# A two-layer graph network on one core: owner matrices kept as bytes, transposes placed behind z, z's weights loaded last

## The chip, the cores and the metric

One Trainium2 chip, one of its cores. The metric is device time in microseconds from the first to the last instruction of the program, with what lies around it; it is given as the median of several runs. A core has TensorE (PE, matrix products; its weight loads are a row of their own, PEld), VectorE (DVE), ScalarE (ACT), GpSimd (POOL) and SyncE (SP). They run side by side, each in the order of its own instructions. DMA transfers are issued from the queues of SP, ACT and POOL.

## The reference

A layer of attention over a graph and a layer of neighbour means, each with a residual sum and a layer norm. There are 4096 nodes with 512 features; `adj` is 4096 x 4096 int32, with about four ones in a row.

```
Wh   = einsum('nf,hfo->hno', x, W)                    # 8 heads of 64
f1   = einsum('hno,ho->hn', Wh, a[:, :64]);  f2 likewise with a[:, 64:]
e    = where(adj > 0, leaky_relu(f1[:, :, None] + f2[:, None, :], 0.2), -9e15)
x1   = layernorm(x + softmax(e) @ Wh)                 # layer 0, heads side by side

agg  = (adj > 0) @ x1 / max(deg, 1)
out  = relu(concat(x1 @ W_self + b_self, agg @ W_nb + b_nb) @ W_comb + b_comb)
y    = layernorm(x1 + out)                            # layer 1
```

## The kernel before, in words

The adjacency is so sparse that the kernel turns each row into a short list of neighbours and gathers rows from DRAM, instead of multiplying with 4096 x 4096 matrices. Nodes are cut into 32 blocks of 128 (`NB`). If a row or a block has more neighbours than the lists hold, a flag sends the program to a dense version, which does not run with these inputs.

Three of a node's neighbours have slots of their own (`K0`). The others of a block share 2 x 128 slots (`KH`): each such slot belongs to one node, its owner. Two 0/1 matrices say who owns what: `of` (kept as bytes for all blocks, slot by node, widened to `st` when used) and the owner matrix `own`, its counterpart, which is made on VectorE when a block needs it: `owners` compares a row of numbers with the owner's number of each slot, twice per block. In layer 1 the same function also scales by 1/degree.

The order of work is written out by hand (`manual_schedule`): every engine runs its instructions in the order in which the Python code issues them. Generators (`decode`, `mean_row`, `fold_weights`) cut longer pieces of work into steps, and `some(...)` or `next(...)` places a step. There are three stages:

1. *Lists and node rows.* For each block b, SyncE loads the adjacency (2 MB in two halves, four buffers `at`), ScalarE turns each half into a 0/1 mask (L379), TensorE folds the masks into keys (`fold_adj`), VectorE takes the largest keys (`max_keys`). Every fourth block a `decode` turns four blocks of keys into neighbour lists `idx` and the `of` matrices (a ScalarE copy to bytes, L470). Beside this `node_block` computes Wh and both attention terms for one block of nodes (L321) and `store` writes them to the DRAM table `t0`. Node blocks run at the pace of the adjacency loop over `LB` = 30 blocks; at b = 12 (`AHEAD`) there is one extra. The two last adjacency blocks and node block 31 are handled after the loop.
2. *Attention.* A software pipeline over i: while block i is normed, block i + 1 is weighed and summed, block i + 2 gets its softmax terms and block i - 1 is multiplied with `m2`. `gather` (L519) issues five indirect DMAs per block from GpSimd, `GA` = 5 blocks deep. On TensorE a block needs: four transposes of its normed rows (`transposed`, L313, then copied by ScalarE, L315), the small products `a_reach` (L569) and `a_shared_sum` (L550), the product with the owner matrix (`a_shared`, L596) and z (`a_z`, L633). z goes to the DRAM table `t1` (L638), 32 stores on SyncE's queue.
3. *Output.* The same kind of pipeline over `t1`, with gathers of five DMAs per block and `GB` = 7 buffers: products with `m1` (L657) and with the scaled owner matrix (L664), ReLU, residual, norm, store.

`m2` and `m1` are products of a weight matrix with its half of `W_comb` (`fold_weights`: four transposes and four products for each of four chunks, L261 and L272). For `m2` the weights (2 MB, `load_fold`) are loaded inside the adjacency loop at b = 28, ahead of adjacency block 30; the fold is spread over the hand-over from stage one to stage two. `fold_bias` (L290) adds four bias terms on VectorE. `m1` is folded between stages two and three.

Around the change, an iteration i of stage two issues, in this order: moments(i), gather(i + 4), transposes(i - 1), reach(i + 1), the widening of `of`, weighing of i + 1, softmax terms of i + 2, root and norm of i, z(i - 1), the rest of the sums of i + 1, the small sum of i + 2, the owner product of i + 1, the owner matrix of i + 3.

In stage three the first gathers stand ahead of the loop:

```
    G1 = {b: gather(t1, b, gps) for b in range(GA)}
    gps += [... for k in range(GA, GB)]
    G1[GA] = gather(t1, GA, gps)
    ...
    for b in range(NB):
        ...
        if b + GB - 1 < NB:
            G1[b + GB - 1] = gather(t1, b + GB - 1, gps)
```

Of the kernel before, what the change touches and what calls it, by code (L numbers as in the profile page):

```python
# [55 lines left out]
GB = 7  # L56
# [31 lines left out]
def listed_layers(  # L88
# [33 lines left out]
    AHEAD = 12  # L122
# [97 lines left out]
    of = const.tile([P, NB, KH * P], U8, name="of")  # L220
    idx = const.tile([P, NB, KS], U32, name="idx")
# [32 lines left out]
    def fold_weights(loaded, m, wp, tag):  # L254
# [12 lines left out]
        for c in range(FB):  # L267
            nxt = turned(c + 1) if c + 1 < FB else None
            yield
            mp = ps.tile([P, HD], F32, name=tag, bufs=2)  # L270
            for d in range(FB):
                nc.tensor.matmul(  # L272
                    mp, lhsT=wT[:, d, :], rhs=wc[:, d, :], start=(d == 0), stop=(d == FB - 1)
                )
            yield
            nc.scalar.copy(m[:, c, :], mp)
            wT = nxt
# [9 lines left out]
    def fold_bias(loaded, bcol):  # L287

        for d in range(FB):
            nc.vector.scalar_tensor_tensor(  # L290
                brow, loaded[1][:, d, :], bcol[:, d : d + 1], brow, OP.mult, OP.add
            )

# [120 lines left out]
    def decode(b0, dp, place, slow=False):  # L414
# [49 lines left out]
        for b in range(b0, b0 + G):  # L464
# [5 lines left out]
            nc.scalar.copy(of[:, b, :], st)  # L470
            sts.append(st)
            if slow or b == b0 + G - 1:
                yield
        pe = ps.tile([P, G, KH, EX + H], F32, name="sm", bufs=2)
# [23 lines left out]
        nc.vector.tensor_scalar(idx[:, bs, K0:KS], jx, float(N + 1), None, OP.min)  # L498

    def owners(b, pool, scaled=False):  # L500

        s = pool.tile([P, KH, P], F32, name="own", bufs=4)
        for k in range(KH):
            E = es[:, b, k, :]
            if scaled:
                nc.vector.tensor_scalar(
                    s[:, k, :], iota[:, 1 : P + 1], E[:, KX + 2 : KX + 3],
                    E[:, KX + 1 : KX + 2], OP.is_equal, OP.mult,
                )
            else:  # L510
                nc.vector.tensor_scalar(
                    s[:, k, :], iota[:, 1 : P + 1], E[:, KX + 2 : KX + 3], None, OP.is_equal
                )
# [16 lines left out]
    def a_owners(b, wp):  # L530
        OWN[b] = owners(b, wp)
# [160 lines left out]
    wp = ctx.enter_context(tc.tile_pool(name="work", bufs=1))  # L692
    dp_cm = tc.tile_pool(name="decode", bufs=1, side="right")
    dp = dp_cm.__enter__()
    fp_cm = tc.tile_pool(name="fold", bufs=1, side="right")
    fp = fp_cm.__enter__()
# [75 lines left out]
    def on_last(b):  # L772
        return sp.tile([P, KH * P], F32, name="last", bufs=G)

    def store(w, row, eng=nc.scalar):
        eng.dma_start(t0[2 + w * P : 2 + (w + 1) * P, :], row[:, 0:TW])
# [5 lines left out]
    for b in range(LB):  # L782
        for k in range(1 + (b == AHEAD)):
            load_x(w + k + XL)
            sum_x(w + k + XL, xacc)
        if b + 2 < LB:
            load_adj(b + 2, ap)
        elif b + 2 == LB:
            loaded = load_fold(1, w_nb, fp)
            load_adj(LB, ap)  # L790
# [6 lines left out]
        nxt = transposed(w + 1, wp)  # L797
# [8 lines left out]
        if b == AHEAD:  # L806
# [10 lines left out]
        if b % G == G - 1:  # L817
            lists = [*lists[-1:], decode(b + 1 - G, dp, on_own)]
    row = node_block(w, xT)
    store(w, row)  # L820
    key_bank(LB)
    for h in range(NH):
        mask_adj(LB, h)
    fold_adj(LB - 1, dp)
    max_keys(LB - 1)
    row = node_block(w + 1, nxt)
    store(w + 1, row, nc.sync)
    load_adj(LB + 1, ap)
# [3 lines left out]
    gps = [ctx.enter_context(tc.tile_pool(name=f"gat{k}", bufs=1)) for k in range(2)]  # L832
    for b in range(2):
        G0[b] = gather(t0, b, gps)
    m2s = fold_weights(loaded, m2, wp, "pw")
    some(lists)
    fold_adj(LB, dp)
    max_keys(LB)
    next(m2s)
    key_bank(LB + 1)  # L840
    some(lists)
    for k in range(3):
        next(m2s)
    mask_adj(LB + 1, 0)
    a_owners(0, wp)
    fold_bias(loaded, bcol)
    some(lists)
    mask_adj(LB + 1, 1)
    next(m2s)
    fold_adj(LB + 1, dp)  # L850
    max_keys(LB + 1)
    next(m2s)
    ap_cm.__exit__(None, None, None)
    bp_cm.__exit__(None, None, None)
    wq = ctx.enter_context(tc.tile_pool(name="work2", bufs=1))
    a_owned(0, wq)
    gps += [ctx.enter_context(tc.tile_pool(name=f"gat{k}", bufs=1)) for k in range(2, GA)]
    sp_cm = tc.tile_pool(name="last", bufs=1, side="right")
    sp = sp_cm.__enter__()
    lists = [decode(NB - G, dp, on_last, slow=True)]  # L860
    some(lists)
# [4 lines left out]
    for i in range(-2, NB + 2):  # L866
# [4 lines left out]
        if on(i - 1):  # L871
            xT = transposed(i - 1, wp)
        if on(i + 1):
            a_reach(i + 1)
        if i == -1:
# [13 lines left out]
        if i == -2:  # L889
            next(m2s)  # L890
            some(lists)
        if on(i):
            norm(i, xs[:, i, :])
        if on(i - 1):
            a_z(i - 1, xT, wp)
        if on(i + 1):
            a_adds(i + 1, wq)
        if on(i + 2):
# [6 lines left out]
        if i == 1:  # L905
            loaded = load_fold(0, w_self, fp)
            brw = load_bias(0)
        if i == -1:
            next(m2s, None)
        if 2 <= i < 12:  # L910
            some(lists)
        if i == 12:
            sp_cm.__exit__(None, None, None)
            m1_pool = ctx.enter_context(tc.tile_pool(name="m1", bufs=1))
            m1 = m1_pool.tile([P, FB, HD], F32, name="m1")
    bcol = bias_column(0, brw)
    fold_bias(loaded, bcol)
    for _ in fold_weights(loaded, m1, wp, "nm"):
        pass
# [3 lines left out]
    fp_cm.__exit__(None, None, None)  # L923
# [6 lines left out]
    for b in range(2):  # L930
        OWN[b] = owners(b, wp, scaled=True)
# [22 lines left out]
    for b in range(NB):  # L954
# [13 lines left out]
        if b + 2 < NB:  # L968
            OWN[b + 2] = owners(b + 2, wp, scaled=True)
# [400 lines left out]
```

## Time and profile before

| | us |
|---|---|
| median of three runs | 802.6 (797.52 to 804.33) |
| the profiled execution, its own time | 717.85 |
| its span | 716.1 |
| TensorE busy | 636.6 (89%) |
| VectorE busy | 492.2 (69%) |
| ScalarE busy | 453.3 (63%) |
| GpSimd busy | 361.6 (50%) |
| mean granted TensorE clock | 0.960 |

The rows of groups give a line of the code, the engine, the operation, what it writes and reads, how often it ran, its busy time, the mean of one in ns, and the idle time of its engine just before, with what ended it. The costliest that the change touches or meets:

```profile
L519 POOL DMA_INDIRECT g<-t,idx x320 | 305.8, 956 | 166.9 <-issue 75.3
L633 PE MATMUL pw<-m,xT 128*128 128x512 f32 x256 | 122.1, 621 | 12.3 <-ACT xT L315 12.3
L315 ACT COPY xT<-tp 128x512 f32<-128x512 f32 x80 | 46.5, 581 | 81.7 <-PE tp L313 80.7
L584 DVE TENSOR_TENSOR g<-g,key 128x1024 f32<-128x1024 f32 x64 | 77.8, 1216 | 1.1
```

A product of 32-bit floats appears as two matmul records, so z's four products are eight rows. In rows of the timeline the columns are start and duration in us, then engine, line and operation; a bracket holds the idle time of that engine just before, and who ended it. The profiled execution is shorter than the runs of the median by 84.75 us.

### The profile page before, as it was taken

To read this page: it belongs to the slowest core of one execution; us is meant where nothing else is said; L and a number is where in the kernel's file an instruction comes from. 1 tells how busy PE (TensorE), PEld (TensorE's weight loads), DVE (VectorE), ACT (ScalarE), POOL (GpSimd) and SP (SyncE) were. 2 spreads that over 40 slices of the span, in tenths; PEclk is the share of its full clock that TensorE was granted. 3 is DMA by queue.
4 is the path that set the end of the run, shared out by engine and by line. 5 is a ranking of instruction groups with operands and counts; after the bars stand their busy time and mean duration, and the time that the engine had idled before them with its cause. 6 is when DMAs were issued, how large, how long until landed. Compare 5 with 4: busy or idle time off the path is not lost. (4 is left out here: it accounts for less than half of the span.)

```text
span 716.1 us, 8935 instructions
## 1 busy us (share of the span) xinstructions
PE 636.6 (89%) x2454; PEld 362.1 (51%) x2454; DVE 492.2 (69%) x1431; ACT 453.3 (63%) x947; POOL 361.6 (50%) x403
## 2 busy tenths in 40 slices
PE   3797898988998789978999999999999999999963
PEld 1565666756665444435555555554444444444421
DVE  5256777766867778999899999983135655666552
ACT  3477786777867526645666575664346876777753
POOL 6512123121000777655576666400777777777771
PEclk9989999999999968999999999999999999999996
DMA  9999999999998878876688878611678888888883
GB/s 280 384 350 393 393 393 394 394 390 392 343 394 305 263 213 275 294 206 189 186 226 231 233 226 234 190 45 44 191 210 261 262 248 256 258 265 249 257 246 119
DMA packets 84262, 191.26 MB, mean 267 GB/s; under 512 B 12513, under 2 KB 12521, under 8 KB 84206
## 3 DMA queue, kind: packets, MB, share of 16 engines
q0 software_dynamic: 25600, 84.56, 40.6%
q1 hardware_dynamic: 53952, 97.53, 37.2%
q10 hardware_dynamic: 4654, 8.54, 3.2%
q8 instruction: 21, 0.34, 0.2%
q14 instruction: 35, 0.29, 0.1%
HBM read 165.29 MB, written 25.31 MB: 266 GB/s over the span
## 5 line engine op out<-in xcount | busy, mean ns | idle before, releaser
L519 POOL DMA_INDIRECT g<-t,idx x320 | 305.8, 956 | 166.9 <-issue 75.3
L379 ACT ACTIVATE ab<-at 128x2048 bf16<-128x2048 int32 x64 | 122.1, 1909 | 43.6 <-DMA at<-in_adj_dram 39.1
L321 PE MATMUL pw<-w_sb,xT 128*128 128x264 f32 x512 | 137.9, 417 | 0.1
L633 PE MATMUL pw<-m,xT 128*128 128x512 f32 x256 | 122.1, 621 | 12.3 <-ACT xT L315 12.3
L321 PEld LDWEIGHTS pw<-w_sb,xT 128*128 128x128 f32 x512 | 99.1, 204 | 29.0 <-issue 3.6
L307 POOL TENSOR_TENSOR xacc<-xacc,xs 128x512 f32<-128x512 f32 x32 | 41.1, 1285 | 123.2 <-DMA xs<-in_x_dram 122.7
L315 ACT COPY xT<-tp 128x512 f32<-128x512 f32 x80 | 46.5, 581 | 81.7 <-PE tp L313 80.7
L633 PEld LDWEIGHTS pw<-m,xT 128*128 128x128 f32 x256 | 47.4, 195 | 63.5 <-issue 48.3
L584 DVE TENSOR_TENSOR g<-g,key 128x1024 f32<-128x1024 f32 x64 | 77.8, 1216 | 1.1
L596 PE MATMUL nm<-g,own 128*128 128x512 f32 x128 | 64.5, 628 | 0.0
L313 PEld LDWEIGHTS tp<-ident,xs 128*128 128x128 f32 x320 | 40.5, 147 | 38.3 <-issue 31.5
L657 PE MATMUL nm<-m,xT 128*128 128x512 f32 x128 | 57.7, 593 | 1.5 <-ACT xT L315 1.5
L313 PE MATMUL tp<-ident,xs 128*128 128x128 f32 x320 | 50.9, 284 | 7.9 <-DMA xs<-in_x_dram 7.4
L657 PE MATMUL pw<-m,xT 128*128 128x512 f32 x128 | 57.6, 592 | 0.0
L325 DVE COPY row<-pw 128x264 f32<-128x264 f32 x64 | 27.1, 424 | 43.1 <-PE pw L321 26.4
L671 DVE SCALAR_TENSOR_TENSOR sm<-y,lst,nm 128x512 f32<-128x512 f32 x16 | 12.1, 755 | 43.7 <-PE nm L664 43.7
L664 PE MATMUL nm<-g,own 128*128 128x512 f32 x64 | 32.0, 625 | 5.9 <-DMA g<-t,idx 5.9
L647 DVE TENSOR_TENSOR sm<-sm,g 128x512 f32<-128x512 f32 x32 | 22.2, 694 | 19.5 <-ACT sm L643 19.5
L657 PEld LDWEIGHTS nm<-m,xT 128*128 128x128 f32 x128 | 23.1, 190 | 24.6 <-issue 23.0
L671 DVE SCALAR_TENSOR_TENSOR sm<-y,lst,pw 128x512 f32<-128x512 f32 x16 | 12.1, 756 | 34.0 <-PE pw L664 34.0
L657 PEld LDWEIGHTS pw<-m,xT 128*128 128x128 f32 x128 | 23.1, 190 | 23.4 <-issue 23.4
L664 PE MATMUL pw<-g,own 128*128 128x512 f32 x64 | 30.3, 595 | 2.0 <-DMA g<-t,idx 2.0
(177 smaller groups left out, 1007.5 us busy)
## 6 DMA issues: line engine op xcount, KB each, us to landing
at<-in_adj_dram SPq DMA_DIRECT2D x64, 1024.0 KB, 10.7
t<-row SPq DMA_DIRECT2D x32, 256.0 KB, 3.5
out_dram<-row SPq DMA_DIRECT2D x32, 256.0 KB, 3.9
t<-row ACTq DMA_DIRECT2D x31, 260.0 KB, 5.8
xs<-in_x_dram SPq DMA_DIRECT2D x31, 256.0 KB, 11.2
g<-t,idx POOLq DMA_INDIRECT x320, 4.2
wc<-in_L_gnn_W_comb_dram SPq DMA_DIRECT2D x2, 1024.0 KB, 16.7
w_sb<-in_L_gnn_W_dram SPq DMA_DIRECT2D x8, 128.0 KB, 4.4
```

The costliest lines, as they stand in the source:

```text
L307: nc.gpsimd.tensor_tensor(xacc, xacc, xs[:, b, :], OP.add)
L313: nc.tensor.transpose(tp[:, c, :], xs[:, b, ts(c, P)], ident)
L315: nc.scalar.copy(t, tp)
L321: nc.tensor.matmul(pw, lhsT=xT[:, c, :], rhs=w_sb[:, c, k * HW : (k + 1) * HW], start=(c == 0), stop=(c == FB - 1),)
L325: nc.vector.tensor_copy(row[:, k * HW : (k + 1) * HW], pw)
L379: nc.scalar.activation(ab, loads.pop((b, h)), AF.Relu, accum_out=asum[:, b, h : h + 1])
L519: nc.gpsimd.indirect_dma_start(out=g[:, k, 0 : table.shape[1]], out_offset=None, in_=table[:, :], in_offset=bass.IndirectOffsetOnAxis(ap=i ...
L584: nc.vector.tensor_tensor(gv if to is None else to.rearrange("p (k h d) -> p k h d", k=1, h=H), gv, E[b][:, sl].unsqueeze(3).to_broadcast( ...
L596: nc.tensor.matmul(NM[b], lhsT=OWN[b][:, k, :], rhs=G0[b][:, K0 + k, H:TW], start=False, stop=(k == KH - 1), skip_group_check=True,)
L633: nc.tensor.matmul(pz, lhsT=xT[:, c, :], rhs=m2[:, c, :], start=(c == 0), stop=(c == FB - 1))
L657: nc.tensor.matmul(NM[b], lhsT=xT[:, c, :], rhs=m1[:, c, :], start=False, stop=False, skip_group_check=True,)
L664: nc.tensor.matmul(NM[b], lhsT=OWN[b][:, k, :], rhs=g[:, K0 + k, 0:HD], start=False, stop=(k == KH - 1), skip_group_check=True,)
```

## The change

- The owner matrices of stage two are no longer made on VectorE for each block. `decode` gets one more step, which makes those of four blocks at once, as bytes (`own`, in a tile that lives through the kernel); `a_owners` is now a ScalarE copy that widens a block's bytes to 32-bit floats. `owners` stays for stage three, always scaled.
- `decode`'s copies to `of` are issued after its loop; for the first six decodes they run on GpSimd, for the last two on ScalarE.
- In stage two the transposes of block i are issued behind z(i - 1) and the sums of i + 1, and used by z(i) in the next iteration. Before, they were issued at the start of the iteration that uses them.
- A second extra node block runs at b = 6, so that all of the loop's blocks end with node block 30, and node block 31 follows directly. All 32 adjacency blocks are loaded in the loop's order; z's weights are loaded behind them. `store` is always on ScalarE's queue.
- `fold_weights` stops after every second product, and its steps are spread over the start of stage two; `fold_bias` stops after every term.
- The last four lists' decode begins earlier, in a tile of the pool of the weights. The weights of `m1` are loaded at i = 12 instead of i = 1, and `m1` is written over the tile of its own weights.
- `GB` is 6 instead of 7. The lines ahead of the loop of stage three that gather blocks 0 to 5 are as before.

```diff
-GB = 7
+GB = 6
-    AHEAD = 12
+    AHEAD = (6, 12)
+    own = const.tile([P, NB, KH, P], U8, name="own8")
@@ fold_weights
-            yield
+                if d % 2:
+                    yield
@@ decode
-            nc.scalar.copy(of[:, b, :], st)
+        for g in range(G):
+            if b0 + G < LB - G:
+                nc.gpsimd.tensor_copy(of[:, b0 + g, :], sts[g])
+            else:
+                nc.scalar.copy(of[:, b0 + g, :], sts[g])
...
+        yield
+        nc.vector.tensor_tensor(
+            own[:, bs].rearrange("p g k c -> p (g k) c"),
+            iota[:, 1 : P + 1].unsqueeze(1).to_broadcast([P, G * KH, P]),
+            es[:, bs].rearrange("p g k c -> p (g k) c")[:, :, KX + 2 : KX + 3].to_broadcast(
+                [P, G * KH, P]
+            ),
+            OP.is_equal,
+        )
@@ a_owners
-        OWN[b] = owners(b, wp)
+        OWN[b] = wp.tile([P, KH, P], F32, name="own", bufs=4)
+        nc.scalar.copy(
+            OWN[b].rearrange("p k c -> p (k c)"), own[:, b].rearrange("p k c -> p (k c)")
+        )
@@ the loop of stage one
-        if b + 2 < LB:
-            load_adj(b + 2, ap)
-        elif b + 2 == LB:
-            loaded = load_fold(1, w_nb, fp)
-            load_adj(LB, ap)
+        load_adj(b + 2, ap)
...
+    loaded = load_fold(1, w_nb, fp)
     row = node_block(w, xT)
     store(w, row)
@@ the hand-over
+    gps = [ctx.enter_context(tc.tile_pool(name="gat0", bufs=1))]
+    G0[0] = gather(t0, 0, gps)
     m2s = fold_weights(loaded, m2, wp, "pw")
     some(lists)
+    for b in (LB, LB + 1):
+        key_bank(b)
+        for h in range(NH):
+            mask_adj(b, h)
+        some(lists)
+        fold_adj(b, dp)
+        max_keys(b)
...
+    lists = [decode(NB - G, dp, on_last, slow=True), *lists[-1:]]
+    for k in range(3):
+        some(lists)
+    for k in range(4):
+        next(m2s)
@@ the loop of stage two
-        if on(i - 1):
-            xT = transposed(i - 1, wp)
...
         if on(i - 1):
-            a_z(i - 1, xT, wp)
+            a_z(i - 1, XT.pop(i - 1), wp)
+        if i == -2:
+            some(lists)
         if on(i + 1):
             a_adds(i + 1, wq)
+        if on(i):
+            XT[i] = transposed(i, wp)
...
+        for k in range({-2: 1, -1: 3, 0: 2}.get(i, 0)):
+            next(m2s, None)
+        if 1 <= i < 12:
+            some(lists)
+        if 1 <= i < 5:
+            next(biased)
+        if i == 12:
+            loaded = load_fold(0, w_self, fp)
+            brw = load_bias(0)
```

## The prediction

> **What bounds the kernel now.** I read the busy time by stage first, then a steady stretch of the second stage in order of time, then the GpSimd queue from 455 us on, then the hand-over between first and second stage. The stages: masks, keys and node rows to 228; hand-over to 274; attention and z to 498; fold of the second weights to 528; output blocks to 716.
>
> ```profile
> core 0: us, PE busy (x) PEld busy (x) DVE busy (x) ACT busy (x) POOL busy (x), PEclk, DMA share, GB/s
> 4.00:228.00 224.00, 191.69 (x1025) 135.58 (x1026) 151.90 (x580) 159.91 (x209) 52.40 (x68) 0.95 1.03 378
> 228.00:274.00 46.00, 37.46 (x125) 20.42 (x123) 34.58 (x103) 20.39 (x45) 32.94 (x34) 0.81 0.77 232
> 274.00:498.00 224.00, 208.62 (x747) 112.66 (x745) 193.80 (x498) 135.33 (x363) 121.18 (x128) 0.99 0.67 200
> 498.00:528.00 30.00, 28.53 (x88) 13.96 (x87) 7.26 (x20) 10.47 (x21) 20.52 (x22) 1.00 0.61 184
> 528.00:716.00 188.00, 170.20 (x475) 79.31 (x473) 102.50 (x218) 125.73 (x310) 131.34 (x139) 0.96 0.77 241
> ```
>
> Stage one is full of DMA (share 1.03). The hand-over leaves TensorE half slow (clock 0.81). In the second stage TensorE (93%) and VectorE (87%) are both nearly full; a steady block shows how they meet:
>
> ```profile
> 411.27 0.60 PE L313 MATMUL tp<-ident,xs 128*128 128x128 f32 x4
> ...
> 411.71 0.51 PE L569 MATMUL sm<-dn,st 128*128 128x8 f32 x4
> ...
> 411.91 0.59 ACT L315 COPY xT<-tp 128x512 f32<-128x512 f32 x1 [2.01 <-PE tp L313]
> ...
> 412.54 3.70 PE L633 MATMUL pw<-m,xT 128*128 128x512 f32 x8 [0.33 <-ACT xT L315]
> ...
> 416.08 0.51 PE L550 MATMUL sm<-e,own 128*128 128x8 f32 x4
> ...
> 416.44 1.96 PE L596 MATMUL nm<-g,own 128*128 128x512 f32 x4
> ...
> 417.92 0.43 DVE L511 TENSOR_SCALAR own<-iota,es 128x128 f32<-128x128 f32 x2
> ...
> 418.25 0.60 PE L313 MATMUL tp<-ident,xs 128*128 128x128 f32 x4
> ...
> 418.44 0.69 DVE L612 SCALAR_TENSOR_TENSOR y<-y,nm 128x512 f32<-128x512 f32 x1
> ```
>
> The period is 418.25 - 411.27 = 6.98 us. TensorE idles 0.33 of it: z needs the ScalarE copy of the transposes, which begins only when they end, and only the small product at 411.71 lies between. VectorE has no gap over 0.1 us, and its last item, the owner matrix, holds it from 417.92 to 418.44, 0.52 us. So two limits of almost one length stand side by side; taking one away alone would gain little.
>
> In stage three the limit is another:
>
> ```profile
> 501.08 0.97 POOL L519 DMA_INDIRECT g<-t,idx  x1 [41.56 <-DVE brow L290]
> 502.35 0.94 POOL L519 DMA_INDIRECT g<-t,idx  x1 [0.30 <-issue]
> ...
> 698.76 3.75 PE L664 MATMUL nm<-g,own 128*128 128x512 f32 x4 [4.97 <-DMA g<-t,idx]
> 704.18 1.96 PE L664 MATMUL pw<-g,own 128*128 128x512 f32 x4 [1.67 <-DMA g<-t,idx]
> ```
>
> GpSimd begins at 501.08, when the last z row is in DRAM (the named releaser had long been done), and issues 160 gathers, one every 1.25 us, without a pause to about 701. TensorE needs 5.59 us for a block (L657 to L657), GpSimd 5 x 1.25 = 6.26. TensorE lives on a head start, and from 679 on it waits for gathers.
>
> **How the profile stands to the median.** The profiled execution took 717.85 us (716.1 of it span); the runs shown have a median of 802.6, 84.75 more. No trace shows where that goes. The row gives a clock of 0.99 to 1.00 in stage two. The Trainium skill ("TensorE: Matmul & The Clock Gate", Part 1) says that a die goes to 13/16 of the clock when three of its cores run dense matmuls, and that one busy core never trips it; so for this program alone the page speaks for the row. If the timed runs had 13/16 all the same (neighbours on the die would do it), an estimate from that page: 6.65 us of TensorE work per block grows by 0.231 x 6.65 = 1.54, x 32 = 49 in stage two, less 6 of stretched blocks that it hides; in stage three 6.88 per block makes TensorE the limit, 32 + 32 x 6.88 + 10 = 262 us after 501 instead of 215, so 47; together about 90. That is so near 84.75 that I take the slower TensorE as the likelier case for the timed runs and make the sum for both.
>
> **The change part by part.**
>
> *Stage two.* (a) The owner matrices leave VectorE (64 x 261 ns at L511, 0.52 us per block with its gap) and become one byte compare per four blocks, 128x1024; nearest row L584, 128x1024, 1216 ns, eight times 10 us, six of them in stage one, where VectorE is 68% busy. Bounds: half and twice that row; I take 1.2, and twice it would still leave stage one's VectorE under 75%. (b) ScalarE gets a widening copy per block: L535, the same shape from bytes, 408 ns. ScalarE is 60% busy here and the copy stands behind the z copy and the transposes' copy; it is needed two blocks later. Cost nothing, covered by about 2.5 us of idle ScalarE per block. (c) Block i's transposes stand behind z of block i-1. Between them and z(i) now lie sum (0.36), the shared product (1.81) and the small product: 2.6 us cover the 0.83 that copy and hand-over take. The 0.33 goes. What is late next: the transposes now need norm(i) at once. Moments end at 419.13; the square began only at 420.19, behind the transposes' copy, which is no longer in front of it, and norm ended 2.64 after that. New end about 0.75 + 0.1 + 2.65 = 3.5 us after the shared product; TensorE reaches the transposes after 0.4 + 3.54 = 3.95. Half a us to spare. New period: TensorE 6.65 less nothing, VectorE 6.46; I take 6.6. Gain 0.38 x 31 = 12 at full clock; 0.3 x 31 = 9 to 10 at 13/16, where the idle copy wait stays as long and is all that can go.
> (d) The decode of the last four lists, the byte compare and the bias products (4 x 0.75, L290) fall into blocks 1 to 11: about 12 us of VectorE work there on a floor of 6.46. Before, the same stretch cost 223 - 31 x 6.98 = 6.6. At full clock that costs 4 more; at 13/16 (period 8.2) it is hidden. Stage two: -8 at full clock, -10 at 13/16.
>
> *First stage and hand-over.* (e) Two blocks run ahead (6 and 12; before, 12 alone), so node block 31 comes before the last fold, and its store is no longer behind masks. Bytes are the same, so the first stage stays bound by DMA: no gain by itself. (f) The byte copies of six decodes go to GpSimd (24 copies; between L332, 226 ns, and L307, 1285 ns: I take 0.6; GpSimd is 23% busy there and only sums of x stand behind). ScalarE loses waits such as these:
>
> ```profile
> 208.96 0.40 ACT L470 CAST of<-own 128x256 uint8<-128x256 f32 x1 [4.04 <-DVE own L469]
> ...
> 249.17 1.02 PE L550 MATMUL sm<-e,own 128*128 128x8 f32 x4 [3.64 <-ACT e L544]
> ...
> 268.66 5.72 PE L633 MATMUL pw<-m,xT 128*128 128x512 f32 x8
> ```
>
> (g) z's weights (2 MB; at 390 GB/s, 5.3 us of the queue) go behind adjacency 30 and 31 on SP, and nothing but z stores follows them there. The last adjacency block, issued at 228.77 before because it stood behind a store, is now issued when its buffers come free, near 220; masks 31 end near 229 to 233 instead of 241.2. The weights then land near 230 to 236 and compete with the first gathers. (h) So the first attention sum, at 249.17 before, can come 7 to 13 us earlier. But the fold (16 products of 0.9, now in halves) lies between the first blocks, and ScalarE's copy of m chunk 2 stands ahead of root(0): chunk 2 ends some 11.5 us after the first sum, moments(0) are ready at 9. From the first sum to the end of z(0) I count 24.5 us at full clock; before it was 274.2 - 249.2 = 25, with z at half speed (5.72 for what takes 3.70 in a steady block). So the hand-over is worth what the first sum gains: -10 at full clock. At 13/16 some 21 us of TensorE work in that chain grow by 3 net: -7. Bounds: 0 (ScalarE or the weights eat it) and -15.
>
> *Stage three.* (i) Six gather buffers instead of seven, but the line that gathers block 5 ahead of the loop stays, and the loop at b = 0 asks for b + 5 = 5 again. The order of GpSimd shows 165 gathers of the second table. Five more cost 5 x 1.25 = 6.3, and the second set writes the tile of the first, so it waits for its landing: 4.2 (median of gathers), of which 1.25 has passed: 3. The page "DMA: Bandwidth & Descriptors" (SWDGE fit) would give 2.0 + 262144/436e3 = 2.6 from issue to landing, so a wait of 1.4; the row decides. Cost at full clock, where GpSimd is the limit: +9.3 (7.7 by the page). At 13/16 GpSimd would end about 225 us after its start and TensorE 262: cost nothing, covered by 37 us. Moving the second weights' load to block 12 and folding them into their own tile costs nothing: they land some 100 us before use.
>
> Sum: full clock -10 - 8 + 9.3 = -9 (717.85 to 709, -1.2%); 13/16: -7 - 10 + 0 = -17 on 802.6: 785.
>
> **The rivals.**
> *Larger gain (773).* The hand-over gives 13 and the steady period falls by 0.5: -29. For it: the first sum's shift of up to 13 and VectorE's 0.52. Against: TensorE's 6.65.
> *It cancels (797).* The hand-over gives nothing, since the fold that used to fill TensorE's holes now stands in the chain of the first blocks, and stage two gives 5. The full-clock sum lands here too: 802.6 - 9 = 794. For it: ScalarE in order behind the copies of m.
> *Slower (811): the gather queue decides the timed runs.* If the 84.75 us lie on GpSimd's 320 gathers, each takes 1.52 instead of 1.25; a block of stage two then takes 7.6 by GpSimd alone, and neither VectorE's nor TensorE's relief counts. Five more gathers cost 7.6 plus a wait of 4, the hand-over brings the first gather perhaps 4 earlier: +8. It decides as soon as five gathers take longer than TensorE's block. For it: at full clock stage three is just so. Against: nothing shows gathers slower than 1.25.
>
> **How the numbers follow.** About 1% (8 us) is what a measurement of this kernel can tell from no change. Forecast (776 to 794) 0.57, larger gain 0.12, cancelling 0.20, slower 0.11. Faster by over 1%: 0.69; within: 0.20; slower: 0.11. The range 766 to 804 leaves out the slower rival, the upper end of the cancelling one and a tip below.
>
> **What would show it.** Steady z to z 6.6 us without a wait of z for xT, and transposes that wait for norm under 0.1 us; L511 gone; the first attention sum near 237 to 242; 165 gathers in stage three and one wait of about 3 us before the 31st. A first sum later than 246, a period above 6.9, or stage three 9 us longer in the timed runs would make it wrong.

## The result, and the profile after

| | before | after |
|---|---|---|
| median, us | 802.97 (796.53 to 808.16) | 796.43 (788.22 to 805.79) |
| ratio to before | | 0.9903 (95% interval 0.9874 to 0.9933) |
| the profiled execution, us | 717.85 | 795.71 |

The change brought 1.0% (6.5 us between the medians; 785 was forecast). One thing must be known to read every number below: this kernel has executions of two kinds, short ones (before near 717 us) and long ones (near 800). Its first profile was of the short kind, the runs behind both medians of the long kind, and so is the profile of after. The kind goes with the session, not with the kernel: all kernels run together showed the same one, and one and the same chip showed the short kind in one session and the long one in another. Each ratio below is against runs of the kernel before made in the same session.

The stages of after (the columns are those of the prediction's first rows; the stages now end at 277, 517 and 540):

```profile
4.00:228.00 224.00, 187.21 (x1026) 131.88 (x1027) 161.44 (x600) 152.53 (x185) 64.95 (x93) 0.98 1.04 382
228.00:277.00 49.00, 33.69 (x117) 18.67 (x114) 25.32 (x77) 17.80 (x39) 30.83 (x32) 0.76 0.67 191
277.00:517.00 240.00, 218.37 (x754) 110.35 (x754) 190.60 (x448) 148.62 (x401) 122.30 (x129) 0.98 0.63 188
517.00:540.00 23.00, 19.62 (x61) 9.59 (x61) 5.35 (x16) 7.20 (x14) 15.02 (x16) 0.96 0.57 173
540.00:794.00 254.00, 198.90 (x505) 91.30 (x503) 104.25 (x222) 127.88 (x317) 141.00 (x150) 0.87 0.62 190
```

The first stage is as it was. The last, 188 us in the short profile, takes 254, and TensorE is busy 78% of it instead of 91%. In stage two the granted clock is 0.98; TensorE is not slow, it stands still. What it stands for is in the waits of after (engine and line, what it waited for, us in total, times, longest):

```profile
ACT xT L318 <- remote: 64.3, 8, 21.2
DVE sm L685 <- remote: 60.5, 7, 10.8
```

"Remote" means that no release on this core explains the end of the wait. One such hole, in the order of time:

```profile
688.15 1.88 PE L678 MATMUL pw<-g,own 128*128 128x512 f32 x4
...
689.87 0.60 PE L316 MATMUL tp<-ident,xs 128*128 128x128 f32 x4
...
694.11 0.95 POOL L530 DMA_INDIRECT g<-t,idx  x1 [0.30 <-issue]
...
695.46 0.60 PE L316 MATMUL key<-ident,xs 128*128 128x128 f32 x4
...
697.96 0.76 DVE L685 SCALAR_TENSOR_TENSOR sm<-y,lst,pw 128x512 f32<-128x512 f32 x1 [10.14 <-remote]
...
698.01 0.58 ACT L318 COPY xT<-tp 128x512 f32<-128x512 f32 x1 [8.88 <-remote]
...
698.66 0.94 POOL L530 DMA_INDIRECT g<-t,idx  x1 [3.60 <-ACT xT L318]
```

ScalarE at 698.01 copies the transposes of 689.87; VectorE at 697.96 takes the product of 688.15, whose four records last 1.88 us. Both start within 0.1 us of each other, 7.5 to 8 us after their matmuls end. TensorE itself went on until its transposes of 695.46 and then stood still. The bracket of GpSimd's last line shows that the gathers then wait as well, for the engines that hold their buffers. The trace's record of TensorE's semaphore shows why they start together:

```
after:             684.46, then 697.85 697.89 697.93 697.99 698.08 698.13 698.17 698.23
before, long kind: 687.52, then 690.31 690.36 690.42 690.51 690.55 690.59 690.65, then 710.72
```

TensorE's updates arrive in a burst, about 0.05 us apart, long after the matmuls. In after, eight TensorE instructions that send an update ended between 688.31 and 696.06, and the burst has eight. The silence of 13.4 us before it is in part a gap of the record: a ScalarE copy at 684.92 follows at once on transposes that ended at 684.88, with no update written down, and between 687.4 and 697.8 us there is no update of VectorE's or ScalarE's own semaphore either, although both ran until 687.8 and 689.1. The traces of short executions have no such burst (four updates or more, each within 0.12 us of the one before); that of after has 12. Those of long ones hold fewer semaphore records of every engine (6320 for after, 11160 for the same program in the short kind), and what is missing lies mostly in stretches ahead of the bursts. So the recording itself may have a part in the holes; no run tests that.

The holes also slow TensorE down afterwards. The first products of a block in the last stage, in after and then in after in a short execution:

```profile
L671 PE MATMUL nm<-wr,xT 128*128 128x512 f32 x128 | 68.4, 684 | 31.1 <-ACT nm L667 25.2
L671 PE MATMUL pw<-wr,xT 128*128 128x512 f32 x128 | 67.7, 678 | 14.6 <-ACT pw L667 10.7
```

```profile
L671 PE MATMUL nm<-wr,xT 128*128 128x512 f32 x128 | 57.7, 593 | 1.5 <-ACT xT L318 1.5
L671 PE MATMUL pw<-wr,xT 128*128 128x512 f32 x128 | 57.6, 592 | 0.0
```

The median is 592 ns in both, but 49 of the 256 products of the long execution take over 0.7 us, most of them 1.06; behind the hole above these are the seven from 699.39 to 705.6. The row of that stretch (columns as in the stages) has half the clock:

```profile
698.60:705.40 6.80, 6.01 (x7) 2.52 (x8) 5.92 (x14) 6.25 (x18) 5.22 (x6) 0.50 0.60 162
```

In the whole stage that adds 20.8 us of TensorE time.

After in a short execution shows what the change itself does. Three groups of its page (busy us and mean ns, then idle time before them):

```profile
L530 POOL DMA_INDIRECT g<-t,idx x325 | 310.0, 954 | 164.9 <-issue 78.7
...
L647 PE MATMUL pw<-m,xT 128*128 128x512 f32 x256 | 117.7, 602 | 0.7 <-ACT xT L318 0.7
...
L318 ACT COPY xT<-tp 128x512 f32<-128x512 f32 x80 | 46.5, 582 | 21.5 <-PE tp L316 20.4
```

And a steady block of it, in the order of time:

```profile
410.60 0.69 DVE L626 SCALAR_TENSOR_TENSOR y<-y,nm 128x512 f32<-128x512 f32 x1 [0.33 <-PE nm L610]
...
410.86 3.68 PE L647 MATMUL pw<-m,xT 128*128 128x512 f32 x8
...
413.46 0.80 ACT L642 ACTIVATE xs<-y,ln_sum,ln_rs 128x512 f32<-128x512 f32 x1
...
414.38 0.60 PE L316 MATMUL tp<-ident,xs 128*128 128x128 f32 x4
...
415.06 0.59 ACT L318 COPY xT<-tp 128x512 f32<-128x512 f32 x1
...
415.18 1.96 PE L610 MATMUL nm<-g,own 128*128 128x512 f32 x4
...
415.54 0.42 ACT L543 CAST own<-own 128x256 f32<-128x256 uint8 x1
...
417.72 0.68 PE L647 MATMUL pw<-m,xT 128*128 128x512 f32 x1
```

z no longer waits for the copy (0.7 us in all, 12.3 before), norm ends at 414.26 and the transposes follow at 414.38, the owner matrix is a ScalarE copy of 0.42 us, and VectorE now has a gap (0.33 us, for the product of the owners). Period: 417.72 - 410.86 = 6.86, the next 6.58, mean 6.72; before, 6.98.

### The profile page after: what moved, and what is told of

Read it like the earlier page. It is cut to its first block, busy times and chain, and to the rows that moved or that the text cites. A ratio compares the mean times of both kernels' runs of the same rounds, so it can differ in the third digit from the quotient of the medians.

```text
span 794.0 us, 8912 instructions
## 1 busy us (share of the span) xinstructions
PE 657.8 (83%) x2454; PEld 361.8 (46%) x2454; DVE 489.1 (62%) x1375; ACT 455.5 (57%) x955; POOL 377.4 (48%) x432
## 3 DMA queue, kind: packets, MB, share of 16 engines
q0 software_dynamic: 26000, 85.87, 37.6%
## 4 chain that ended last, share of the span: by engine, by line
PE 37%; another core or an unknown queue 8%; issue 4%; DVE 4%; ACT 2%; DMA 1%; POOL 0%; DVEq 0%; POOLq 0%; ACTq 0%
PE pw L647 10%; PE nm L610 6%; PE pw L671 5%; PE nm L671 5%; PE tp L316 2%; PE nm L678 2%; PE pw L678 2%; PE nm L273 1%; PE sm L583 1%; DMA g<-t,idx 1%; DVE sm L685 1%; PE sm L564 1%; DVE y L663 1%; DVE sm L661 0%
## 5 line engine op out<-in xcount | busy, mean ns | idle before, releaser
L324 PE MATMUL pw<-w_sb,xT 128*128 128x264 f32 x512 | 133.7, 407 | 5.4 <-DVE row L328 4.0
L647 PE MATMUL pw<-m,xT 128*128 128x512 f32 x256 | 119.5, 610 | 0.7 <-ACT xT L318 0.7
L671 PE MATMUL nm<-wr,xT 128*128 128x512 f32 x128 | 68.4, 684 | 31.1 <-ACT nm L667 25.2
L671 PE MATMUL pw<-wr,xT 128*128 128x512 f32 x128 | 67.7, 678 | 14.6 <-ACT pw L667 10.7
L647 PEld LDWEIGHTS pw<-m,xT 128*128 128x128 f32 x256 | 46.8, 193 | 48.4 <-issue 47.3
L610 PE MATMUL nm<-g,own 128*128 128x512 f32 x128 | 65.2, 634 | 0.0
L671 PEld LDWEIGHTS nm<-wr,xT 128*128 128x128 f32 x128 | 26.7, 219 | 61.8 <-issue 35.6
L328 DVE COPY row<-pw 128x264 f32<-128x264 f32 x64 | 27.1, 424 | 38.3 <-PE pw L324 21.9
L633 ACT ACTIVATE xs<-y,ln_sum 128x512 f32<-128x512 f32 x32 | 23.1, 723 | 47.7 <-DVE y L626 33.8
L671 PEld LDWEIGHTS pw<-wr,xT 128*128 128x128 f32 x128 | 26.8, 220 | 44.7 <-issue 33.2
L318 ACT COPY xT<-key 128x512 f32<-128x512 f32 x16 | 9.3, 582 | 65.4 <-remote 36.5
```

Of the source, the lines that this page charges most:

```text
L318: nc.scalar.copy(t, tp)
L324: nc.tensor.matmul(pw, lhsT=xT[:, c, :], rhs=w_sb[:, c, k * HW : (k + 1) * HW], start=(c == 0), stop=(c == FB - 1),)
L610: nc.tensor.matmul(NM[b], lhsT=OWN[b][:, k, :], rhs=G0[b][:, K0 + k, H:TW], start=False, stop=(k == KH - 1), skip_group_check=True,)
L647: nc.tensor.matmul(pz, lhsT=xT[:, c, :], rhs=m2[:, c, :], start=(c == 0), stop=(c == FB - 1))
L671: nc.tensor.matmul(NM[b], lhsT=xT[:, c, :], rhs=m1[:, c, :], start=False, stop=False, skip_group_check=True,)
```

## The experiments

**Which kind is the kernel before?** Unchanged, profiled in two further sessions.

> The kernel before, unchanged, profiled once more, because its first profiled execution (717.85 us) is 85 us shorter than all its other runs. Theory of the prediction (TensorE at 13/16 of its clock in the other runs): about 800 us, with z's eight records at 4.5 us instead of 3.7 and a granted clock near 0.81 in stage two. Rival (stalls): about 800 us, z's records still 3.7 us at a granted clock of 1.0, and some 60 to 90 us in holes of several us in which ScalarE, VectorE and TensorE stand still although the producer ended long before, as in the trace of after.

> The kernel before, unchanged, one look, for a trace of it in the long kind of execution if that is the kind that is met: then stage two near 240 us and stage three near 275 as in the kernels derived from it and in after, no z slower than 3.7 us, TensorE's semaphore updates in bursts after pauses of 5 us and more. If the short kind is met: as the first such look, 713 to 718.

The first met the short kind (715.3 us), the second the long one (791.6). In the long one the largest waits that its short profile does not have are

```profile
DVE sm L671 <- remote: 72.8, 8, 10.7
ACT xT L315 <- remote: 61.5, 10, 10.5
```

z's matmuls have a median of 592 ns there, as in after, and the stages read (before in a long execution):

```profile
279.00:515.00 236.00, 215.32 (x753) 114.49 (x752) 197.32 (x506) 138.58 (x371) 122.51 (x129) 0.99 0.65 191
...
540.00:790.00 250.00, 187.25 (x490) 86.56 (x488) 104.25 (x222) 126.93 (x316) 134.96 (x143) 0.88 0.60 185
```

Holes, not a slow clock: the rival named in the first expectation holds.

**Short executions: the parts of the change.** "Once" stands for after without the second gathering of block 5:

```diff
-        if b + GB - 1 < NB:
+        if 0 < b and b + GB - 1 < NB:
             G1[b + GB - 1] = gather(t1, b + GB - 1, gps)
```

The transposes back in the old place (o_tr0; b_tr is the reverse, on the kernel before):

```diff
+        if on(i - 1):
+            XT[i - 1] = transposed(i - 1, wp)
         if on(i + 1):
             a_reach(i + 1)
...
-        if on(i):
-            XT[i] = transposed(i, wp)
```

The owner matrices back on VectorE (o_dve; a_old2 has both, with block 5 gathered twice as in after):

```diff
-        nc.scalar.copy(
-            OWN[b].rearrange("p k c -> p (k c)"), own[:, b].rearrange("p k c -> p (k c)")
-        )
+        for k in range(KH):
+            nc.vector.tensor_scalar(
+                OWN[b][:, k, :], iota[:, 1 : P + 1], es[:, b, k, KX + 2 : KX + 3], None,
+                OP.is_equal,
+            )
```

The weights from ScalarE's queue, behind the last row's store (o_wact):

```diff
-    loaded = load_fold(1, w_nb, fp)
     row = node_block(w, xT)
     store(w, row)
+    loaded = load_fold(1, w_nb, fp, nc.scalar)
```

> The kernel before with one part of the change: in stage two the transposes of block i stand behind z of block i - 1. Prediction's terms: little alone, since VectorE, still with the owner matrices, is full in the same period: 0 to -4 us. If TensorE's wait for the copy of the transposes also sits in the long runs: up to -10. If the transposes wait for norm as they do in the trace of after (16.8 us in all): 0 to +8.

> After with stage two as before: owner matrices on VectorE for each block, transposes at the start of the iteration that uses them; what is left of the change are the first stage, the hand-over, the weights loaded last and six gather buffers. Prediction: stage two is worth 8 to 10 us of the change, so this is 8 to 10 us slower than after, 804 to 806. Rival (stage two gives its gain back in waits for norm): within 3 us of after, 794 to 799. If it is slower than the kernel before, hand-over and the gathers done twice cost.

> After without gathering block 5 of the second table a second time (160 gathers instead of 165 in stage three). Prediction: at full clock the five gathers and their wait cost 9.3 us, with TensorE as the limit nothing. Gather-bound stage three: 787. TensorE- or stall-bound stage three: 794 to 797, as after.

> After, unchanged, beside the kernel before. If the ground state is the 717 us of the last runs (no holes of several us), the pieces seen so far give: hand-over 3 to 6 us earlier, stage two 7.5 us shorter, stage three 10 to 11.5 us longer for the five gathers done twice, so 714 to 718, a ratio of 0.995 to 1.002; the prediction's sum for the full clock said 709, a ratio of 0.987. If the holes are there (before near 800), the ratio is again near 0.990.

> After without the second gathering of block 5, and with the transposes of stage two back at the start of the iteration that uses them; owner matrices stay bytes widened on ScalarE. If the order of the transposes is what stage two gains from and the owner matrices bring little alone: z to z 6.9 to 7.0 us, stage two 4 to 6 us longer than with both parts, ratio to the kernel before 0.986 to 0.990 (with both: 0.981). If VectorE was the limit: z to z 6.7, ratio 0.981 to 0.983.

> After without the second gathering of block 5, and with the owner matrices of stage two made on VectorE for each block again; transposes stay behind z. The kernel before with the transposes alone had z to z 6.79 us; so 6.8 here, 2 us longer in the steady part and 1 to 2 us in the blocks that share VectorE with the last decode, less the 1.2 us byte compare: ratio 0.983 to 0.987 (with both parts 0.981).

> After without the second gathering of block 5, and with z's weights loaded from ScalarE's queue behind the store of the last node row instead of from SyncE's queue ahead of it. Theory: the store took 6.6 us to the first gather because 2 MB of weights stood before it in the DMA engines (3.2 us before the change); then the first gather comes at 228 to 229 instead of 231.6, the first attention sum 2 to 3 us earlier and the whole 2 to 3 us shorter, ratio 0.977 to 0.979. Rival: the products of the fold set the hand-over, or the weights now come late; first z at 265 or later, ratio 0.980 to 0.984.

Measured (us of one trace each: start of the first z, from there to the end of the last z, from there to the end of the span; ratio with its interval):

| kernel | first z | stage two | the rest | ratio to before |
|---|---|---|---|---|
| before (b_again) | 268.6 | 226.8 | 218.2 | 1 |
| transposes moved alone (b_tr) | 269.1 | 222.9 | 217.9 | 0.9935 (0.9916 to 0.9954) |
| after (a_again) | 266.3 | 219.5 | 230.0 | 0.9985 (0.9967 to 1.0003) |
| after, stage two as before (a_old2) | 262.9 | 225.1 | 229.9 | 1.0035 (1.0018 to 1.0051) |
| once (a_once) | 265.3 | 219.3 | 219.7 | 0.9807 (0.9785 to 0.9829) |
| once, old place of transposes (o_tr0) | 263.1 | 224.1 | 218.1 | 0.9905 (0.9888 to 0.9923) |
| once, owners on VectorE (o_dve) | 263.1 | 222.8 | 220.2 | 0.9854 (0.9837 to 0.9872) |
| once, weights behind the store (o_wact) | 265.5 | 219.1 | 219.8 | 0.9853 (0.9832 to 0.9874) |

The three kernels o_tr0, o_dve and o_wact ran in another session than once. The trace of o_wact agrees with that of once within 0.2 us in each column, and its ratio is 0.005 higher all the same; so parts of this size are read from the columns, not from ratios of different sessions.

So in short executions the change is worth nothing, as a sum of two sides. Stage two is 7.3 us shorter: the transposes alone bring 3.9, with a z every 6.79 us. With the bytes alone (o_tr0) a z still comes every 6.98 us, so TensorE's wait was the tighter of the two limits; both together give 6.72. The gathers done twice cost 10.3 in the last stage. GpSimd's row at that place, in after:

```profile
525.83 0.95 POOL L530 DMA_INDIRECT g<-t,idx  x1 [0.30 <-issue]
...
530.64 0.95 POOL L530 DMA_INDIRECT g<-t,idx  x1 [3.87 <-DMA g<-t,idx]
```

The 31st gather waits 3.87 us for the landing of the 26th to 30th, which fill the same tile and of which the last was issued at 525.83; five gathers of 1.25 and this wait of 3.57 beyond the usual 0.30 make 9.8.

The hand-over gave 2.3 instead of 10. The first attention sum of the kernel before (b_again), and then the hand-over of after (short):

```profile
249.89 0.86 PE L550 MATMUL sm<-e,own 128*128 128x8 f32 x4 [3.76 <-ACT e L544]
```

```profile
240.40 0.59 ACT L278 COPY m<-pw 128x512 f32<-128x512 f32 x1 [3.16 <-PE pw L273]
...
242.89 0.61 PE L564 MATMUL sm<-e,own 128*128 128x8 f32 x4 [2.09 <-ACT e L558]
...
252.86 0.64 DVE L626 SCALAR_TENSOR_TENSOR y<-y,nm 128x512 f32<-128x512 f32 x1
...
255.83 0.59 ACT L278 COPY m<-pw 128x512 f32<-128x512 f32 x1 [2.79 <-PE pw L273]
...
257.14 0.72 ACT L633 ACTIVATE xs<-y,ln_sum 128x512 f32<-128x512 f32 x1
...
266.27 3.68 PE L647 MATMUL pw<-m,xT 128*128 128x512 f32 x8
```

The first sum comes at 242.89, 7 us before that of the kernel before. Moments(0) end at 253.5, but the square of root(0) stands on ScalarE behind the copy of the fold's third product, which waits for TensorE until 255.8. From the first sum to the start of the first z it is 23.4 us, before 18.7. In o_wact the first gather came 2.2 us earlier than in after (229.24, 231.45), and the first sum not at all (243.78): there the copy of the fold's first product (to 243.1) stood before the first softmax terms. Its theory fell.

**The hand-over put in another order**, each with block 5 gathered once: the copy behind root(0) (first diff), that with the weights behind the store, and that with half a chunk of the fold moved behind the first softmax terms.

```diff
-        if -1 <= i < 1:
+        if i == -1:
             next(m2s)
-        if i == 0:
-            next(m2s)
...
             norm(i, xs[:, i, :])
+        if i == 0:
+            next(m2s)
+            next(m2s)
```

```diff
-    for k in range(4):
+    for k in range(2):
         next(m2s)
...
-        for k in range({-2: 1, -1: 3, 0: 2}.get(i, 0)):
+        for k in range({-2: 3, -1: 3, 0: 2}.get(i, 0)):
```

> After without the second gathering of block 5, and with ScalarE's copy of the fold's third product (and the first half of the fourth) placed behind root and norm of block 0 instead of ahead of them. Theory: in the hand-over root(0) stands on ScalarE behind that copy (moments at 252.5, root at 256.2); without it norm(0) ends about 3 us earlier, the first z starts 2 to 3 us earlier (262.5 to 263.5 for masks that end at 234) and the whole is 2 to 3 us shorter: ratio to the kernel before 0.977 to 0.980. Rival: TensorE itself, with 64 product records of the fold, sets the first z; then nothing is gained, 0.981 to 0.985.

> As o_root, and z's weights loaded from ScalarE's queue behind the last node row's store (alone that brought the first gather 2 us forward and nothing else). If root(0) was what hid it: another 1 to 2 us, ratio 0.975 to 0.978. If the first chunk of the fold, ahead of the first softmax terms on ScalarE, hides it still: as o_root.

> As o_rootw, and only half of the fold's first chunk ahead of the first softmax terms; its other half and its copy behind them. Theory: the first attention sum comes at 240 to 241 instead of 243.6, and the first z 4 to 5 us earlier than in after without the second gathering (260 to 261): ratio 0.973 to 0.976. Rival: TensorE's work in the hand-over is what counts, only its order changes: as o_root, 0.977 to 0.981.

Only long executions were met: 0.9932 (0.9905 to 0.9958), 0.9980 (0.9952 to 1.0009), 0.9965 (0.9921 to 1.0008). Their first z comes at 276.5, 286.8 and 284.5, where once alone has 285.6 and after 277.0; their hand-over has waits of 13.6, 12.8 and 13.5 us whose end nothing on this core explains. Whether the order would help in a short execution stays open.

**Long executions: what is the 1% made of?** Six buffers and nothing else, that with block 5 gathered once, five buffers, and after gathering once:

```diff
-GB = 7
+GB = 6
```

```diff
-GB = 7
+GB = 5
-    G1[GA] = gather(t1, GA, gps)
-        if b + GB - 1 < NB:
+        if 0 < b and b + GB - 1 < NB:
```

> The kernel before with six gather buffers instead of seven in stage three and nothing else; block 5 of the second table is then gathered twice, as in after. Prediction's term: five gathers of 1.25 us and a wait of 3: +9.3 us, ratio 1.013. Measured in after without it: 10 to 12.8 us, ratio 1.014 to 1.018. If the executions have the holes of several us (before near 800): 0 to +3 us, ratio 1.000 to 1.004, since the gathers then have slack.

> The kernel before with six gather buffers and block 5 gathered twice, once more: 0.9935 in the long executions. In the short ones, by the prediction's term of 9.3 us, 1.013; by what after loses there, 1.014 to 1.018.

> The kernel before with six gather buffers instead of seven in stage three, and block 5 gathered once (160 gathers). If the buffer itself is what made the kernel before faster in the long executions (ratio 0.9935 with six buffers and 165 gathers): 0.990 to 0.995 there. If the five gathers done twice made it faster there: 0.998 to 1.002. In the short executions (before near 717): 0.999 to 1.003 by every theory, since the gathers run without a pause either way.

> The kernel before with five gather buffers in stage three, each block gathered once. In long executions six buffers alone gave 0.995; if fewer gathers on the way shorten the holes, five give 0.985 to 0.993; if six was only a matter of placement, 0.995 to 1.005. In short executions (before near 717) the gathers of a block must wait for the buffer of the block just used: 1.000 to 1.020.

> After without the second gathering, once more: in the short executions it had a ratio of 0.981 (after itself 0.9985). In the long ones (before near 800) after has 0.990. If the gathers done twice are covered there, as the prediction had it: 0.988 to 0.992. If they cost what they cost in the short ones: 0.975 to 0.980. If they bring something there: 0.994 to 0.998.

Here "gathers" is the time from the first to the last gather of the second table, and "tail" what follows the start of the last one; both are part of the rest. The trace of a_once_2 took 804.3 us, 6.5 more than its median.

| kernel, long executions | stage two | the rest | gathers | tail | ratio to before |
|---|---|---|---|---|---|
| before (b_again_2) | 235.9 | 275.3 | 234.0 | 37.6 | 1 |
| six buffers (b_gb6_2; the first ratio is b_gb6) | 236.2 | 273.3 | 240.5 | 29.2 | 0.9935 (0.9910 to 0.9960), 0.9942 (0.9917 to 0.9966) |
| six, block 5 once (b_six_once) | 240.9 | 272.6 | 240.0 | 29.0 | 0.9949 (0.9923 to 0.9976) |
| five, block 5 once (b_five) | 240.2 | 265.3 | 238.4 | 23.2 | 0.9851 (0.9786 to 0.9916) |
| after | 239.8 | 277.3 | 239.8 | 33.8 | 0.9903 (0.9874 to 0.9933) |
| after, block 5 once (a_once_2) | 240.9 | 276.1 | 238.8 | 33.7 | 0.9930 (0.9892 to 0.9969) |

The buffer is the largest piece that an experiment shows: six instead of seven give 0.6% in the kernel before, with the second gathering or without, and five give 1.5%. The first expectation had seen no gain there. It does not lie in shorter holes, as the expectation for five buffers had it: in the kernels made from before the gathers take 4 to 6 us longer with fewer buffers, and the tail is shorter by 8 and 14 us (one trace each; after, with six, has a tail of 33.8). Stage two shows no gain: 236 to 241 us with the old order and with the new.

The second gathering costs nothing that can be told here (0.9942 against 0.9949; 0.9903 against 0.9930), and the traces show what covers it. The 31st gather of a_once_2, and then the 31st and the 36th of after (the first of block 6):

```profile
581.61 0.95 POOL L530 DMA_INDIRECT g<-t,idx  x1 [14.19 <-PE key L316]
```

```profile
561.34 0.94 POOL L530 DMA_INDIRECT g<-t,idx  x1 [3.73 <-issue]
...
573.23 0.94 POOL L530 DMA_INDIRECT g<-t,idx  x1 [5.95 <-PE key L316]
```

Every long execution has a hole at the start of the last stage that holds the gathers. The five repeated ones run inside it: from the start of the 30th gather to the first of block 6 it is 15.1 us without them and 16.6 with them. In short executions there is no such hole, and they cost their full 9.8.

**What sets the pace?** Four gathers for a block in the last stage instead of five:

```diff
-    def gather(table, b, pools):
+    def gather(table, b, pools, n=KS):
...
-        for k in range(KS):
+        for k in range(n):
...
-                NM[b], lhsT=OWN[b][:, k, :], rhs=g[:, K0 + k, 0:HD],
+                NM[b], lhsT=OWN[b][:, k, :], rhs=g[:, K0, 0:HD],
...
-            G1[b + GB - 1] = gather(t1, b + GB - 1, gps)
+            G1[b + GB - 1] = gather(t1, b + GB - 1, gps, KS - 1)
```

> After without the second gathering, and with four gathers per block instead of five in stage three; the fifth slot's product reads the fourth's rows, so the output is not the reference's. Theory for long executions (the rival that the gather queue decides): first to last gather took 240 us there in every kernel, 1.5 us for each of 160, in stage two as in stage three; then 128 take 192, and stage three is some 45 us shorter: 750 to 756. Rival (the holes come once in so many us and have nothing to do with the number of gathers): stage three falls only by what it falls in short executions. In short executions GpSimd needs 5.0 us for a block, TensorE 5.6: TensorE becomes the limit, stage three about 32 x 5.6 + 20 = 200 instead of 220: 684 to 688.

748.66 us, ratio 0.9416 (0.9364 to 0.9468). From the first to the last gather of the second table a_once_2 takes 238.8 us for 160, this kernel 194.4 for 128: 1.50 and 1.53 us for each on the mean. The last stage falls from 276.1 to 228.2. Its row (from 540 to the end, TensorE 87% busy, where after had 78%):

```profile
540.00:750.00 210.00, 182.41 (x506) 85.66 (x506) 104.87 (x222) 128.76 (x320) 110.06 (x117) 0.94 0.62 188
```

The mean hides what happens. Around one hole GpSimd's row reads, in a_once_2 and then in this kernel:

```profile
680.50 0.95 POOL L530 DMA_INDIRECT g<-t,idx  x1 [0.30 <-issue]
685.04 0.95 POOL L530 DMA_INDIRECT g<-t,idx  x1 [3.58 <-ACT xT L318]
```

```profile
671.99 0.95 POOL L530 DMA_INDIRECT g<-t,idx  x1 [0.30 <-issue]
675.95 0.94 POOL L530 DMA_INDIRECT g<-t,idx  x1 [3.01 <-ACT xT L318]
```

Between such holes a gather starts every 1.25 us, as in short executions. In the steady part the holes are three blocks apart: after 15 gathers and 22.1 us in a_once_2, after 12 gathers and 17.7 us here. Beyond 1.25 us for each gather they take 39.6 us there and 35.6 here. So of the 44 us by which the stretch of gathers is shorter, 40 are 32 gathers at 1.25 us and only 4 are smaller holes. Holes that come by the clock are excluded, since they come sooner here; but the gathers have no price of 1.5 us either, as the theory had it, and its number, 750 to 756, came out near the measured one because most of the 1.5 is the 1.25. TensorE also gains: of its 256 first products only 6 take over 0.7 us here, 47 in a_once_2. What it is in three blocks that brings a hole, no run shows.

## Why the prediction was wrong, step by step

- **How the profile stands to the median: the step that failed.** It took the 84.75 us for a TensorE at 13/16 of its clock. In long executions of before and after z's matmuls take 592 ns, the granted clock is 0.98 to 0.99 in stage two, and the time is in holes behind late semaphore updates. The model also put the time in the wrong place: 43 of its 90 us lie in stage two and 47 behind it, while the two later traces of before differ by 9 us in stage two, 57 behind it and 10 ahead of it. The 17 us forecast, -10 from stage two and -7 from the hand-over, rested on that model; neither shows in the long traces. The page "TensorE: Matmul & The Clock Gate" of the Trainium skill, quoted there for saying that one busy core does not trip the slow clock, agrees with these 0.98 to 0.99; I set it aside because 90 us of a model lay near 84.75. A sum that fits a missing time is no evidence for its cause.
- **(c) and stage two at 13/16, -10:** the mechanism came as drawn (z's wait for xT 0.7 us, no wait ahead of the transposes in the steady block), and at full clock the size too (-7.3 for -8; period 6.72 for 6.6). In the long executions it is worth nothing that the traces show: with the holes a z comes every 7.50 us in the steady blocks of after and every 7.30 in those of before (17 blocks of one trace each). That the holes swallow the gain is argued from this, not shown by a run.
- **(a), (b):** right. The byte compare took 1.22 us; the widening copy cost nothing; alone it leaves the period at 6.98.
- **(d):** mis-sized. The blocks beside the decode cost 10.4 us over nine steady periods of 6.72; before, 9.4 over eleven of 6.98. One us more, not four, since the prediction had put the old share at 6.6.
- **(g), (h), -10 or -7:** wrong in short executions, 2.3. The first sum came 7 us earlier, at the lower end of the 7 to 13. The 24.5 us counted from the first sum to the end of z(0) were 27.1, and the 25 of the kernel before were 22.4 in its next short execution, where z(0) ran in 3.70 us instead of 5.72. The copy of the fold ahead of root(0), which the text named, held root(0) back by 3.6 us. In long executions the first z lies between 276 and 287 in old and new kernels alike.
- **(i), +9.3 or 0:** right on both sides. 10.3 us in short executions, with a wait of 3.87 where 3 was said; nothing in the long ones, though not because TensorE is the limit there: the hole at the start of the stage covers them.
- **Six buffers:** counted only for the gather they repeat. That fewer buffers shorten a long execution (4.6 us, from the mean ratio of 0.9942) was no term of the sum, and it is most of the 6.5; the rest of these is not told apart from noise.
- **The rivals.** "Slower" had the right mean, 1.52 us for each gather, but by luck: the gathers still come every 1.25 us, with holes between. It was right that neither VectorE's nor TensorE's relief counts there, for another reason than its own. Its sum failed, because the five further gathers cost nothing. "It cancels" has the right number (797), by other terms; that is luck too.

Open: why the updates come late, whether the recording has a part in it, why the holes of the last stage are three blocks apart, and why fewer buffers shorten the tail by more than they lengthen the gathers.

After with block 5 gathered once gives 0.9807 in short executions and 0.9930 in long ones, where it cannot be told from after itself. Of the versions measured in both kinds it is the best. Five buffers on top of it were not tried.

## What to carry to other kernels

When the profiled execution is 10% shorter than the runs it stands for, the first question is what the others do, and a second profile answers it; a model that fills the gap does not. An index that is asked for twice at the seam between a prologue and its loop costs a whole round of the engine that is the limit, and nothing where it isn't. A mean time per transfer is not its price: look at the gaps from one to the next before building on it, for here 1.5 us was 1.25 us and a hole every three blocks.

## What the runs showed of the hardware

- The same program took 715.6 us (after) or 796.4, with the same median durations of its instructions: z 592 ns, the gather's instruction 0.95 us. The packets of the gathers' queue took 41.7% of 715.8 us and 37.6% of 794.0, 298 us both times: the transfers are not slower either. TensorE's semaphore updates come late, in bursts about 0.05 us apart (12 in after, none in the same program in the short kind). VectorE's and ScalarE's records show no burst, but a quarter to a third of them is missing.
- Behind a hole TensorE's products took 1.06 us instead of 0.59, at a granted clock of 0.50, for 6.8 us in the one shown.
- Fewer buffers can be faster: with seven, six and five gather buffers a long execution took 1, 0.994 and 0.985 of the time. The cause is open.
